# Scores chained in PSUM by key differences, in a differential-attention and ternary feed-forward block

## The chip, the cores and the metric

The kernel runs on one core of a Trainium2 chip. The metric is device time in microseconds. Five engines matter: PE (TensorE, matrix products), DVE (VectorE), ACT (ScalarE), POOL (GpSimd), and SP (SyncE), which issues the DMAs. PE writes its results into eight PSUM banks of 128 x 512 fp32 values; ACT and DVE read them. Each engine works through its own queue in order and waits on semaphores for the others.

## The reference

The input x has 8 batches of 1024 tokens with 512 features. Two residual blocks follow one another:

```python
qkv = layernorm(x) @ w_qkv                       # 16 heads of 32 features
q1, q2 = split(q); k1, k2 = split(k)             # 16 features each
a1 = softmax(q1 @ k1.T / sqrt(32)); a2 = softmax(q2 @ k2.T / sqrt(32))
out = (a1 - lam * a2) @ v                        # per head
out = out / rms(out) * norm_w * (1 - 0.8)
x = x + reorder(out) @ wo
h = bitlinear(layernorm(x), w_fc) + gate * (low-rank term)
x = x + bitlinear(relu(h) ** 2, w_proj)          # weights rounded to -1, 0, 1 times a scale
```

Everything is fp32. The kernel's products of scores use a pair of rounded numbers for each fp32 number (a high part and the rest), laid along the contracted rows.

## The kernel before

A **unit** is one head of one batch for half of the queries (512): 256 units in all, 32 a batch. A unit has eight **key blocks** of 128 keys, and the main loop runs over them two at a time, so a **step** is two blocks and a unit is four steps (`kc` = 0, 2, 4, 6). Everything is computed transposed: a score bank holds 128 keys by 512 queries of one of the two softmax halves (`sm` 0 and 1).

Two streams run beside each other. `max_scores` (L200) computes, 16 blocks ahead (`AHEAD`, L443), the scores with queries along the partitions, and DVE reduces every bank to its negated row maximum (L223). There are four such products and four reductions in a step. The maxima of a unit are turned by PE (`max_turn`, L241, with a transpose at L243), split into high part and rest on DVE, and sent through DRAM into the tile `nms`. `exp_scores` (L264) then computes the scores of a block: first a product of ones with `nms`, which writes minus the maximum into the bank, and then the product of keys and queries on top of it; ACT takes the exponential out of the bank (L284). Each of these products uses 64 of PE's 128 rows, half 0 the lower and half 1 the upper rows, and neighbours of different halves overlap. `values` (L307) multiplies the exponentials of the step before with V, `add_up` (L290) adds them on POOL, and `sums` (L321) turns the sums into denominators on PE.

PSUM's eight banks are three in a ring for the maxima (`ps_mx`, L60), four in a ring called `one` (L61) for the scores and for every other product, and one accumulator. In a step the four maximum products therefore need the first one's bank again for the fourth. In the first call of a step (`apart=True`) ACT copies the first bank to SBUF (L218), and DVE reduces the copy later, after the others.

The order on PE, ACT, DVE and POOL is the program's order; nothing is reordered. In a step the program emits: the first maximum product, the four products of one block with the second maximum product behind them, the four of the other block, POOL's addition, two more maximum products, the **128-row work** that is due, DVE's last reductions, the values, and then the `post` functions (the ACT and DVE work on the results of the 128-row work), in the order in which they were collected.

The 128-row work is: the preparation of the next batch (`prepare`, L410: normalized tiles turned by `advance`, V by `value_tile`, queries and keys by `project`, L152), `max_turn`, the unit's result turned back and normalized (`heads_out`, L329), `sums`, and once in four units the RMS norm (L367 to L384) and the product with `wo` (`output_rows`, L386). One preparation step is taken at `kc` = 0 of each unit, and an extra one at `kc` = 4 of every fourth unit in a batch's second half; a turned tile and a V tile alternate in the first half, and projections follow. A projection is eight matmuls and has a post: ACT writes the high part (L165), DVE the rest (L166), SP stores both into `qk` in DRAM. `load_keys` (L178) and `load_queries` (L187) bring a head's rows back, each doubled. In the last batch there is no next one to prepare; every second unit there (`light`) leaves its last addition to PE. After the attention loop the feed-forward part runs over 16 groups of 512 tokens.

Of the kernel before, what the change touches and what calls it, by code (L numbers as in the profile page):

```python
# [24 lines left out]
def block_phases(  # L25
# [30 lines left out]
    p_mc = ctx.enter_context(tc.tile_pool(name="a_mc", bufs=2))  # L56
    p_tk = ctx.enter_context(tc.tile_pool(name="a_tk", bufs=3))
# [45 lines left out]
    hT_of, v_of, qk_of, og_of = {}, {}, {}, {}  # L103
# [7 lines left out]
    def begin_batch(b):  # L111
        hT_of[b] = big.tile([P, KC, S], F32, tag="hT", name="hT")
        v_of[b] = big.tile([P, NS, E], F32, tag="v", name="v", bufs=2)
        qk_of[b] = dpool.tile([2, E, 2, S], F32, tag="qk", name="qk", bufs=2)

# [36 lines left out]
    def project(b, which, blk, half):  # L152
# [9 lines left out]
        def post():  # L162
# [6 lines left out]
            nc.sync.dma_start(qk_of[b][which, blk * P : (blk + 1) * P, :, tok], pc.bitcast(F32))  # L169
# [4 lines left out]
    tk_of, tq_of = {}, {}  # L174

    def load_keys(g):  # L178
        b, h = divmod(g, H)
        tk_of[g] = p_tk.tile([P, S], F32R, tag="tk", name="tk")  # L180
        src = qk_of[b][1, h * HD : (h + 1) * HD]
        for i in range(2):
            nc.sync.dma_start(
                tk_of[g][i::2].bitcast(F32), src[:, i : i + 1, :].to_broadcast([HD, 2, S])
            )
# [11 lines left out]

    copy_of = {}

    def max_scores(u, i, apart=False):  # L200
# [15 lines left out]
        if apart:  # L216
            copy_of[0] = p_mc.tile([P, 512], F32, tag="mc", name="mc")
            nc.scalar.copy(copy_of[0], mx[0])  # L218
        else:
            product(1)  # L220

        def reduce(kh, sm, src):
            nc.vector.tensor_reduce(  # L223
                nm_of[u][:, kh, sm, c : c + 1], src, AX.X, ALU.max, negate=True
            )

        def post():
            for sm in range(1 if apart else 0, 2):
                reduce(kh, sm, mx[sm])
            if not apart and copy_of:  # L230
                reduce(0, 0, copy_of.pop(0))
# [32 lines left out]
    def exp_scores(u, kc, between=None):  # L264


        if kc % 2 == 0:
            e_of[u, kc // 2] = p_e.tile([P, 2, 2, HS], F32, tag="e", name="e")
        e = e_of[u, kc // 2]
        halves = (1, 0) if between else (0, 1)  # L270
        st = {sm: one_bank() for sm in halves}
        for w, m, cols in (
            (one2, nms[u % 3], slice(0, P)),
            (tk_of[u // 2], tq_of[u], slice(kc * P, (kc + 1) * P)),
        ):
            for sm in halves:
                rows = slice(64 * sm, 64 * sm + 64)
                nc.tensor.matmul(  # L278
                    st[sm], w[rows, cols], m[rows, :], start=(w is one2), stop=(w is not one2)
                )  # L280
        if between:
            between()
        for sm in halves:
            nc.scalar.activation(e[:, kc % 2, sm, :], st[sm], AF.Exp)  # L284
# [22 lines left out]
    def values(u, kc):  # L307
        b, h = divmod(u // 2, H)
        if kc == 0:
            acc_of[u] = ps_acc.tile([P, 512], F32, tag="acc", name="acc")[:, 0 : HS // 2]  # L310
        quarters(
            acc_of[u], v_of[b][:, kc, h * HD : (h + 1) * HD], e_of[u, kc // 2][:, kc % 2],
# [8 lines left out]
    def sums(u):  # L321
        ps = one_bank()
# [87 lines left out]
    def prepare(b):  # L410
# [15 lines left out]
        steps = [(start, False), (lambda: advance(-2), False), (lambda: advance(-1), False)]  # L426
        for t in range(NS):
            steps += [(lambda t=t: advance(t), False), (lambda t=t: value_tile(b, t), True)]
        return steps + [
            (lambda w=which, k=blk, f=half: project(b, w, k, f), True)  # L430
# [12 lines left out]
    AHEAD = 16  # L443
# [7 lines left out]
    with tc.tile_pool(name="a_stage", bufs=1) as stage, tc.manual_schedule(engines=engines):  # L451
# [55 lines left out]
        for i, step in enumerate(steps):  # L507
# [4 lines left out]
            now = [others.pop(0) for _ in range(2 if i < heads + 2 else 1) if others]  # L512
# [8 lines left out]
            if i == heads - 3:  # L521
                load_keys(0)
                load_queries(0)
            if i >= heads:
                um, im = divmod(i - heads, NS)
                if im == 0:
                    if um > 0:
                        load_keys(um // 2 + 1)
# [40 lines left out]
    def prepare_tokens():  # L569
# [24 lines left out]
        return [(lambda i=i: step(i), False) for i in range(-2, 4)]  # L594
# [4 lines left out]
    for v in range(NU):  # L599
        adds.setdefault((v + 1, 2) if light(v) else (v + 2, 0), []).append(v)  # L600
# [524 lines left out]
```

## Time and profile before

| | us |
|---|---|
| median of 3 runs | 5311.46 (5309.91 to 5316.05) |
| the profiled execution's own time | 5314.59 |
| its span | 5312.1 |
| PE busy | 5212.4 |
| POOL busy | 4125.0 |
| DVE busy | 3818.4 |
| ACT busy | 3311.5 |

The span runs from the first to the last instruction; the time around it is the launch. Busy time is the union of an engine's rows: overlapping matmuls count once. The attention loop runs from about 140 to 4236 us, the feed-forward part from there to the end. The profiled core had its full clock for 0.998 of the time. Of one batch (the transposes of the maxima, L243, mark the units) the length is 518.5 to 518.8 us; units of the second half last 15.5, 15.9, 15.6 and 22.6 us in turn, the last with output rows and an extra projection. A row of a group gives busy time, mean length of one in ns, and the engine's idle time just before them with what ended it. A row of the timeline gives start, length, engine, line, operation, and how many were merged.

### The profile page before, as it was taken

The numbers are of one execution on the slowest core, as the hardware profiler recorded it, in microseconds if no ns is written. First come the engines' busy times: TensorE is split into PE (matmuls) and PEld (weight loads), VectorE is DVE, ScalarE is ACT, GpSimd is POOL, SyncE is SP. The second block draws the span as 40 slices with busy tenths as digits, with TensorE's granted clock in tenths as the row PEclk, the third lists the DMA queues.
The fourth block names the chain that finished last, engine by engine and source line by source line (L and its number), as shares of the span: only waits on it lengthen the run. The fifth ranks groups of instructions, "written<-read, shape, count | busy, mean of one in ns | idle before, by whom it ended". The sixth has DMA issues, their size and how long they took to land.

```text
span 5312.1 us, 106552 instructions
## 1 busy us (share of the span) xinstructions
PE 5212.4 (98%) x41522; PEld 3200.8 (60%) x41522; DVE 3818.4 (72%) x7599; ACT 3311.5 (62%) x6518; POOL 4125.0 (78%) x1495
## 2 busy tenths in 40 slices
PE   8999999999999999999999999999999999999999
PEld 4555555555555555555555555555555588888887
DVE  6877787777778777877787778777888645555554
ACT  4776777677767776777677767776777622222221
POOL 0898899889989998999899989998888733333333
PEclk9999999999999999999999999999999999999999
DMA  8112211221121112111211121112211101111111
GB/s 275 48 55 76 71 50 56 75 70 52 56 79 64 52 56 77 64 56 60 77 60 53 65 73 62 52 66 77 97 50 46 60 19 32 32 32 32 32 32 32
DMA packets 185252, 328.54 MB, mean 62 GB/s; under 512 B 33312, under 2 KB 55840, under 8 KB 184112
## 3 DMA queue, kind: packets, MB, share of 16 engines
q1 hardware_dynamic: 183824, 319.12, 18.5%
q8 instruction: 330, 5.41, 0.4%
q0 software_dynamic: 544, 2.10, 0.1%
q14 instruction: 170, 1.39, 0.1%
q10 hardware_dynamic: 384, 0.52, 0.0%
HBM read 209.16 MB, written 112.46 MB: 61 GB/s over the span
## 4 chain that ended last, share of the span: by engine, by line
PE 84%; POOL 8%; ACT 5%; issue 2%; DVE 1%; DMA 0%; SPq 0%; POOLq 0%; DVEq 0%; ACTq 0%
PE acc L301 16%; PE one L278 14%; PE mx L210 12%; PE y L774 8%; PE one L158 8%; PE pf L755 8%; PE one L301 5%; POOL es L296 4%; ACT e L284 4%; PE one L146 4%; PE one L394 4%; PE one L335 2%; POOL es L294 2%; PE pf L759 1%; ACT mc L218 1%
## 5 line engine op out<-in xcount | busy, mean ns | idle before, releaser
L296 POOL TENSOR_TENSOR es<-es,e 128x2048 f32<-128x2048 f32 x495 | 2263.9, 4574 | 51.6 <-ACT e L284 19.7
L223 DVE TENSOR_REDUCE nm<-mx 128x1 f32<-128x512 f32 x3080 | 1990.6, 686 | 319.8 <-PE mx L210 258.4
L284 ACT ACTIVATE e<-one 128x512 f32<-128x512 f32 x4096 | 2132.1, 615 | 24.4 <-PE one L278 15.9
L294 POOL TENSOR_TENSOR es<-e 128x2048 f32<-128x2048 f32 x256 | 1170.9, 4574 | 259.3 <-ACT e L284 259.3
L210 PE MATMUL mx<-tk,tq 64*128 64x512 f32 x4096 | 1362.9, 421 | 1.1 <-DVE nm L223 0.4
L278 PE MATMUL one<-nms,one 64*128 64x512 f32 x4096 | 1177.7, 421 | 31.7 <-ACT e L284 28.5
L301 PE MATMUL acc<-e,v 128*32 128x256 f32 x16384 | 1093.9, 384 | 0.0
L278 PE MATMUL one<-tq,tk 64*128 64x512 f32 x4096 | 1061.5, 392 | 0.0
L210 PEld LDWEIGHTS mx<-tk,tq 64*128 64x128 f32 x4096 | 701.7, 184 | 490.3 <-DVE nm L223 284.9
L218 ACT COPY mc<-mx 128x512 f32<-128x512 f32 x1016 | 598.8, 589 | 311.2 <-PE mx L210 284.4
L764 POOL TENSOR_TENSOR r<-r 128x512 f32<-128x512 f32 x256 | 268.5, 1050 | 640.0 <-ACT r L763 619.8
L301 PEld LDWEIGHTS acc<-e,v 128*32 128x32 f32 x16384 | 451.6, 109 | 443.6 <-issue 166.5
L223 DVE TENSOR_REDUCE nm<-mc 128x1 f32<-128x512 f32 x1016 | 687.2, 676 | 0.0
L763 ACT ACTIVATE r<-pf,s_fc 128x512 f32<-128x512 f32 x256 | 176.4, 689 | 795.4 <-PE pf L759 558.3
L278 PEld LDWEIGHTS one<-tq,tk 64*128 64x128 f32 x4096 | 581.4, 185 | 80.0
L278 PEld LDWEIGHTS one<-nms,one 64*128 64x128 f32 x4096 | 517.3, 184 | 109.5 <-ACT e L284 56.9
L774 PE MATMUL y<-wpr,r 128*128 128x512 f32 x2048 | 524.9, 398 | 3.5 <-DVE r L767 1.5
L767 DVE CAST r<-r 128x512 fp32r<-128x512 f32 x256 | 180.7, 706 | 424.6 <-POOL r L764 422.2
L158 PE MATMUL one<-hT,wqk 128*128 128x512 f32 x1024 | 474.4, 606 | 2.0 <-ACT hT L139 1.5
L774 PEld LDWEIGHTS y<-wpr,r 128*128 128x128 f32 x2048 | 375.8, 188 | 98.7 <-DVE o L784 20.1
L755 PE MATMUL pf<-hTh,wfc 128*128 128x512 f32 x1024 | 398.9, 390 | 0.0
L755 PE MATMUL pf<-hTl,wfc 128*128 128x512 f32 x1024 | 398.7, 389 | 0.0
(139 smaller groups left out, 4562.4 us busy)
## 6 DMA issues: line engine op xcount, KB each, us to landing
qk<-pc SPq DMA_DIRECT2D x128, 512.0 KB
tq<-qk SPq DMA_DIRECT2D x512, 128.0 KB
tk<-qk SPq DMA_DIRECT2D x256, 256.0 KB
xs<-in_L_attn_x SPq DMA_DIRECT2D x64, 256.0 KB
xr<-in_L_attn_x SPq DMA_DIRECT2D x256, 64.0 KB
x_dram<-y SPq DMA_DIRECT2D x64, 256.0 KB
out<-o SPq DMA_DIRECT2D x248, 64.0 KB
nms<-md SPq DMA_DIRECT2D x512, 4.0 KB
```

The source lines that it names most:

```text
L158: nc.tensor.matmul(ps, wqk[:, kc, c0 : c0 + P], hT_of[b][:, kc, tok], start=(kc == 0), stop=(kc == KC - 1),)
L210: nc.tensor.matmul(mx[sm], tq[rows, c * P : (c + 1) * P], tk[rows, kh * 512 : kh * 512 + 512], start=True, stop=True,)
L218: nc.scalar.copy(copy_of[0], mx[0])
L223: nc.vector.tensor_reduce(nm_of[u][:, kh, sm, c : c + 1], src, AX.X, ALU.max, negate=True)
L278: nc.tensor.matmul(st[sm], w[rows, cols], m[rows, :], start=(w is one2), stop=(w is not one2))
L284: nc.scalar.activation(e[:, kc % 2, sm, :], st[sm], AF.Exp)
L294: nc.gpsimd.tensor_add(es_of[u], e_of[u, 0], e)
L296: nc.gpsimd.tensor_add(es_of[u], es_of[u], e)
L301: nc.tensor.matmul(out[32 * g : 32 * g + 32, :], w, e[:, g // 2, (g % 2) * (HS // 2) : (g % 2 + 1) * (HS // 2)], start=start, stop=stop,)
L755: nc.tensor.matmul(pf, w[:, kc, :], hT, start=(kc == 0 and i == 0), stop=False)
L764: nc.gpsimd.tensor_mul(r, r, r)
L774: nc.tensor.matmul(ys[i], r2[:, i * P : (i + 1) * P], prep.wpr[j // (NJ // 2)][:, j % (NJ // 2), :], start=(j == 0 and k == 0), stop=(j == ...
```

## The change

Minus the maxima are multiplied only for a unit's first two blocks. The other six blocks are computed on top of what their bank already holds: the bank of block i holds the scores of block i - 2 minus the maximum, and a product of the queries with the **difference of the keys** of the two blocks turns it into the scores of block i minus the maximum. For that, blocks are taken in the order 0, 4, 1, 5, 2, 6, 3, 7 (`block`), so that both chains go through neighbouring blocks of one half of the keys. A projection of keys now also stores differences: its post copies the product to SBUF, subtracts it shifted by 128 columns, splits the difference into a high part and the rest, and stores these and the first blocks themselves into a second DRAM array, `kd`. `load_steps` brings a head's differences into `td`, once in two units, beside the keys `tk` that the maxima still use.

Since the four banks of `one` now hold scores from a unit's first block to its last, other work can use them only at the unit's end (`kc` = 6): preparation, `max_turn`, `heads_out` and most `sums` go there, and the loads of a next tile (`"pre"`) to `kc` = 2. What must be done elsewhere (output rows, the sums of light units) takes a bank of the maxima's ring. Where more than three posts wait, the first is done ahead of `sums`. The copy of a maximum bank on ACT is gone: DVE reduces all four from PSUM. The maxima run 18 blocks ahead.

```diff
-    p_mc = ctx.enter_context(tc.tile_pool(name="a_mc", bufs=2))
-    p_tk = ctx.enter_context(tc.tile_pool(name="a_tk", bufs=3))
+    p_tk = ctx.enter_context(tc.tile_pool(name="a_tk", bufs=2))
...
-            nc.sync.dma_start(qk_of[b][which, blk * P : (blk + 1) * P, :, tok], pc.bitcast(F32))
+            rows = slice(blk * P, (blk + 1) * P)
+            nc.sync.dma_start(qk_of[b][which, rows, :, tok], pc.bitcast(F32))
+            if which == 0:
+                return
+            kf = p_x.tile([P, E], F32, tag="x", name="kf")
+            nc.scalar.copy(kf, ps)
+            pd = p_pc.tile([P, 2, HS], F32R, tag="pc", name="pd")
+            hi, lo = pd[:, 0, P:], pd[:, 1, P:]
+            nc.vector.tensor_sub(lo.bitcast(F32), ps[:, P:], kf[:, 0 : HS - P])
+            nc.scalar.copy(hi, lo.bitcast(F32))
+            nc.vector.tensor_sub(lo, lo.bitcast(F32), hi.bitcast(F32))
+            k0 = half * HS
+            nc.sync.dma_start(kd_of[b][rows, :, k0 : k0 + P], pc[:, :, 0:P].bitcast(F32))
+            nc.sync.dma_start(kd_of[b][rows, :, k0 + P : k0 + HS], pd[:, :, P:].bitcast(F32))
...
+    def load_steps(g):
+        b, h = divmod(g, H)
+        td_of[g] = p_tk.tile([P, S], F32R, tag="td", name="td")
+        load_doubled(td_of[g], kd_of[b][h * HD : (h + 1) * HD])
...
         product(0)
-        if apart:
-            copy_of[0] = p_mc.tile([P, 512], F32, tag="mc", name="mc")
-            nc.scalar.copy(copy_of[0], mx[0])
-        else:
+        if not apart:
             product(1)
...
         def post():
-            for sm in range(1 if apart else 0, 2):
-                reduce(kh, sm, mx[sm])
-            if not apart and copy_of:
-                reduce(0, 0, copy_of.pop(0))
+            for sm in range(2):
+                nc.vector.tensor_reduce(
+                    nm_of[u][:, kh, sm, c : c + 1], mx[sm], AX.X, ALU.max, negate=True
+                )
...
+    def block(i):
+        return (i % 2) * (NS // 2) + i // 2
...
         halves = (1, 0) if between else (0, 1)
-        st = {sm: one_bank() for sm in halves}
-        for w, m, cols in (
-            (one2, nms[u % 3], slice(0, P)),
-            (tk_of[u // 2], tq_of[u], slice(kc * P, (kc + 1) * P)),
-        ):
+        first = i < 2
+        if first:
+            st_of[i] = {sm: one_bank() for sm in halves}
+        st = st_of[i % 2]
+        cols = slice(block(i) * P, (block(i) + 1) * P)
+        if first:
             for sm in halves:
                 rows = slice(64 * sm, 64 * sm + 64)
                 nc.tensor.matmul(
-                    st[sm], w[rows, cols], m[rows, :], start=(w is one2), stop=(w is not one2)
-                )
+                    st[sm], one2[rows], nms[u % 3][rows, :], start=True, stop=False
+                )
+        for sm in halves:
+            rows = slice(64 * sm, 64 * sm + 64)
+            nc.tensor.matmul(
+                st[sm], td_of[u // 2][rows, cols], tq_of[u][rows, :], start=False, stop=True,
+                skip_group_check=not first,
+            )
...
-    AHEAD = 16
+    AHEAD = 18
...
-        adds.setdefault((v + 1, 2) if light(v) else (v + 2, 0), []).append(v)
-        outs.setdefault((v + 2, 0) if light(v) else (v + 3, 0), []).append(v)
+        adds.setdefault((v + 1, 2) if light(v) else (v + 1, 6), []).append(v)
+        outs.setdefault((v + 1, 6) if light(v) else (v + 2, 6), []).append(v)
...
-            if fill and (kc == 0 or kc == 4 and u % (2 * H) >= H and u % 4 == 0):
-                prepare_step, long = fill.pop(0)
...
-                    later[u, 6] = lambda n=n: rms_squares(n)
-                    later[u + 1, 0] = lambda n=n: rms_sums(n)
-                    later[u + 1, 2] = lambda n=n: rms_apply(n)
-                    later[u + 2, 4] = lambda n=n: output_rows(n)
...
+            if kc == 2 and u < NU:
+                if u % 2 == 0 and u + 2 < NU:
+                    load_steps(u // 2 + 1)
+                if fill and fill[0][1] == "pre":
+                    fill.pop(0)[0]()
+            if kc == 6:
+                if fill and fill[0][1] == "long":
+                    posts.append(fill.pop(0)[0]())
+                if um <= NU:
+                    posts.append(max_turn(um - 1))
+                for v in outs.pop((u, kc), []):
+                    posts.append(heads_out(v))
+                    if v % 4 == 3:
+                        n = v // 4
+                        later[u + 1, 2] = lambda n=n: rms_squares(n)
+                        later[u + 1, 4] = lambda n=n: rms_sums(n)
+                        later[u + 2, 0] = lambda n=n: rms_apply(n)
+                        later[u + 2, 4] = lambda n=n: output_rows(n, mx_bank)
+                if fill and fill[0][1] == "turn":
+                    posts.append(fill.pop(0)[0]())
...
             if reduce:
                 reduce()
+            if len(posts) > 3:
+                posts.pop(0)()
+            for v in adds.pop((u, kc), []):
+                posts.append(sums(v, one_bank if kc == 6 else mx_bank))
```

In the feed-forward part the tile `r2` alternates between the tags `tk` and `td`, four buffers instead of three.

## The prediction

> **What bounds the kernel now.** I read the page's busy line first, then the groups by shape for the two things the change touches, then the busy time of two stretches, then the timeline.
>
> ```profile
> PE 5212.4 (98%) x41522; PEld 3200.8 (60%) x41522; DVE 3818.4 (72%) x7599; ACT 3311.5 (62%) x6518; POOL 4125.0 (78%) x1495
> L223 DVE TENSOR_REDUCE nm<-mx 128x1 f32<-128x512 f32 x3080 | 1990.6, 686 | 319.8 <-PE mx L210 258.4
> L278 PE MATMUL one<-nms,one 64*128 64x512 f32 x4096 | 1177.7, 421 | 31.7 <-ACT e L284 28.5
> ```
>
> PE looks like the only bound, and the products with the maxima (L278, `nms`) cost it 1177.7 us of overlapped rows. That is the tempting reading. The stretches below are the two halves of one batch of the attention loop (16 units each); columns are length, then PE, PEld, DVE, ACT and POOL busy.
>
> ```profile
> 3226.00:3470.00 244.00, 237.34 (x2226) 134.51 (x2227) 197.40 (x406) 189.54 (x374) 238.73 (x84) 1.00 0.17 51
> 3470.00:3742.00 272.00, 271.60 (x2304) 152.22 (x2304) 202.51 (x407) 188.19 (x375) 237.78 (x61) 1.00 0.24 81
> ```
>
> In the first half POOL is busy 238.7 of 244 us: its three 4.6 us additions a unit are the bound. In the second PE is (271.6 of 272), because every unit carries a projection. Only there can PE time be won.
>
> The inside of one step (two key blocks; four steps make a unit):
>
> ```profile
> 2029.10 0.50 PE L210 MATMUL mx<-tk,tq 64*128 64x512 f32 x1
> 2029.10 0.74 PE L278 MATMUL one<-nms,one 64*128 64x512 f32 x2
> 2029.64 0.59 ACT L218 COPY mc<-mx 128x512 f32<-128x512 f32 x1
> 2030.15 1.95 DVE L223 TENSOR_REDUCE nm<-mx 128x1 f32<-128x512 f32 x3
> 2030.39 0.39 PE L210 MATMUL mx<-tk,tq 64*128 64x512 f32 x2
> 2030.71 1.07 PE L301 MATMUL acc<-e,v 128*32 128x256 f32 x16
> 2031.71 0.50 PE L210 MATMUL mx<-tk,tq 64*128 64x512 f32 x1
> ```
>
> A step lasts 2031.71 - 2029.10 = 2.61 us (2.59 to 2.61 elsewhere). Its twelve 64-row products run as six overlapping pairs: the first takes 0.34, the next 0.23 each, so the last two maximum products start at 1.29 (1.26 in other steps); the values start 0.32 later and take 1.0. DVE is nearly as full: four reductions spaced 0.60 to 0.66 give 2.4 to 2.6. What a maximum bank costs when a reduction frees it is seen once, at the loop's start:
>
> ```profile
> 138.71 0.72 PE L210 MATMUL mx<-tk,tq 64*128 64x512 f32 x2
> 139.24 1.29 DVE L223 TENSOR_REDUCE nm<-mx 128x1 f32<-128x512 f32 x2 [1.88 <-PE mx L210]
> 139.98 0.18 PEld L210 LDWEIGHTS mx<-tk,tq 64*128 64x128 f32 x1 [0.52 <-DVE nm L223]
> ```
>
> Product at 138.71, reduction at 139.24 (0.53 later), its first 0.686 done at 139.93, next product into that bank at 139.98 (0.05 later): 1.27 us from a product to the next in the same bank. Last, a unit's end with a projection:
>
> ```profile
> 2036.92 0.27 PE L243 MATMUL one<-ident,nm 128*8 128x128 f32 x1
> 2037.12 0.60 ACT L165 ACTIVATE pc<-one 128x512 fp32r<-128x512 f32 x1 [2.32 <-PE one L158]
> 2037.76 0.69 DVE L166 SCALAR_TENSOR_TENSOR pc<-one,pc 128x512 fp32r<-128x512 f32 x1 [2.48 <-ACT pc L165]
> 2038.36 0.27 DVE L247 CAST mt<-one 8x128 fp32r<-8x128 f32 x1
> 2039.43 0.49 PE L210 MATMUL mx<-tk,tq 64*128 64x512 f32 x1
> 2039.80 0.29 DVE L358 TENSOR_TENSOR og<-one,o 128x128 f32<-128x128 f32 x1
> ```
>
> The next unit starts 2.51 us after the projection's last issue (2036.92), and DVE is free of the posts only 0.66 us after that start.
>
> **The change part by part.**
>
> *Products with the maxima.* 3072 of 4096 go, six pairs a unit, in three of its four steps. Taken from PE's rows alone: 2 x 0.23 = 0.46 us a step, 768 steps, 353 us.
>
> *The ACT copy of one maximum bank (L218) goes, the ring stays at three banks.* A step uses four: the fourth product goes into the first one's bank. Before, that bank was free at 0.53 + 0.59 = 1.12 (ACT), and PE came at 1.26: no wait. Now PE comes at 0.34 + 2 x 0.23 = 0.80, but the bank is free only after the reduction: 0.53 + 0.69 + 0.05 = 1.27. So PE waits 0.47 there, and with it the values queued behind: 1.27 + 0.32 + 1.0 = 2.59 us a step. The saving of 0.46 becomes this wait. DVE keeps up (four reductions at 0.605 = 2.42, plus 0.17 for L235 in one step). I take 0 for the mid-steps; the ends are 0 and -0.46. ACT's 0.59 a step is off the path: four exponentials at 0.52 are 2.07.
>
> *Key differences, in the eight projections of keys per batch.* The post becomes on DVE and ACT: L166, a subtraction from PSUM, a rounding copy on ACT, a second subtraction, and only then the posts of the maxima and of the heads, queued on DVE behind them. Not in the trace at 384 columns; between 256 and 512 columns the rows are 0.42 and 0.69 (DVE), 0.38 and 0.59 (ACT). Middle values: 0.56 + 0.05 + 0.48 + 0.05 + 0.48 (the second at DVE's spacing) = 1.62 later, ends 1.3 and 2.1. DVE is then free 0.66 + 1.62 = 2.28 after the next unit's start, and the fourth product comes at 2.26 + 0.69 + 0.05 = 3.0 instead of 1.27: 1.74 us. (The heads' bank, needed by the next unit's fourth score bank, comes free at 2.3, inside this wait.) Before, the first reduction of a step was of a late copy and nothing waited for it. 8 x 1.74 = 13.9 a batch. For queries' projections DVE is free at 0.66, product at 1.40: 8 x 0.13 = 1.0.
>
> *Moved work.* L373 (0.68) now sits between a mid-step's reductions: the next first reduction is 0.57 late, six times in a batch's heavy units: 3.4. The output rows' bank comes from the three-bank ring, 0.2 x 6 = 1.2. `rms_apply` moves on POOL ahead of another unit's additions, its 4.2 us unchanged; sums come one step earlier, so POOL may lag 2.6 us less.
>
> *Distribution.* All long work is now at unit ends, one a unit: 24 units in a row with it, 8 without. Heavy: 3 x 2.59 + 1.67 to the projection + 3.54 + 2.5 = 15.48; 24 x 15.48 + 8 x 0.5 (four L138 transposes) + 6 x 3.7 (eight L394 matmuls at 0.43 and the switch) = 397.7. The same count for the old second half (16 x 15.48 + 3 x 3.54 + 4 x 3.7 = 273) meets its 272 to 273.5. Light: a unit without a projection is 3 x 2.59 + 1.67 + 2.5 = 11.94 on PE, so 8 x 12.0 + 2 x 3.7 = 103; POOL needs 8 x (3 x 4.6 + 4.2/4) = 119 (L379, L380 and L382 together 4.2, once in four units) plus 3 of statistics, less what it may lag behind; I take 115, nearer POOL's end because the first half above runs at POOL's pace. Sum 512.7, against 518.6 measured between batch starts: -5.9.
>
> *Queues.* SP gets 256 more loads (`td`, 256 KB like `tk`) and 128 more stores of some 0.55 us of issue; the last store of a key projection holds SP 1.6 us longer, with the maxima's store and the queries' load behind it, both due a unit later. The engines' DMA share of 0.17 to 0.24 has room for 96 MB more: 0. If that cover went, each late load would cost a unit its wait of a microsecond or two.
>
> *Sum.* A batch: -5.9 + 13.9 + 1.0 + 3.4 + 1.2 = +13.6. Seven batches prepare another: +95. The last one has no projections but eight of each moved wait: 8 x 0.57 + 8 x 0.2 = +6. The feed-forward part is untouched. The profiled run's own 5314.6 (span 5312.1 and 2.5 around it) + 101 = 5415.6; it lies 3.1 above the median, so **5412 us**.
>
> [...] With the copy kept the fourth product would come at 1.17 by the rows, 0.10 a step better: some 50 us over 24 x 3 x 7 steps.
>
> **The rivals.**
>
> *The key posts don't show* (chance 0.17). DVE idles about 5 us of each projection, which speaks for it; against it, that idle time lies before the projection ends, and the posts need its result. Without 7 x 13.9: 5314, from 5285 to 5345 with the light stretch at 103 to 119.
>
> That the products would not really go is no rival: their loop runs only for a unit's first two blocks.
>
> *The fourth product does not wait* (0.13, the faster side). If its bank were free at 0.80, 0.46 goes from three steps in 24 units: 33 a batch, 7 x (13.6 - 33) = -136, and 32 x 1.38 = -44 plus 6 in the last: 5311 - 174 = 5137. It decides from 0.2 us a step: the product would have to come by about 1.07. DVE's own 2.42 a step leaves only 0.17 of it. Against it stands the one direct reading of 1.27.
>
> *More waits at unit ends* (0.12). If POOL's shorter slack or late maxima cost each unit of a batch 0.4 us more: 5412 + 7 x 32 x 0.4 = 5502. For it: POOL already has 98% in half the units.
>
> **How the numbers follow.** The forecast has 0.58; alone it reaches from 5350 (light stretch 107, key posts 1.3) to 5465 (light 119, posts 2.1). The range takes in the first rival: 5285 to 5490, leaving out the faster case and most of the slowest, 0.2. About 0.2% (5301 to 5322) is what can be told from no change. Faster: 0.13 + 0.05 of the first rival = 0.18; same 0.07; slower 0.75.
>
> **What would show it.** Right: the fourth L210 product of a step 1.27 after the first, waiting for DVE's reduction; steps still 2.6; units after a key projection some 1.7 longer; PE busy falling while its waits for the reductions grow. Wrong: steps near 2.15 to 2.45, or key units no longer than query units. The light stretch (the POOL floor) is the weakest term.

## The result, and the profile after

The changed kernel takes 5845.87 us (median of four runs, 5838.94 to 5848.15) against 5313.2 us for the kernel before (four runs): a ratio of 1.1001, 95% interval 1.0982 to 1.1020. It is slower, as forecast, but by 533 us where 101 were forecast, and far above the range. Its profiled execution took 5846.1 us (span 5844.3), at a mean granted clock of 0.958 instead of 0.998.

From the page of the kernel after: the busy line, and the groups of the reductions, of the products with the maxima and of the output rows; the last line is the output rows of the kernel before. A group row gives busy time, mean ns of one, and the idle time before them with what ended most of it.

```profile
PE 5425.4 (93%) x38450; PEld 3049.7 (52%) x38450; DVE 3980.1 (68%) x7727; ACT 2890.2 (49%) x5630; POOL 4119.7 (70%) x1495
...
L242 DVE TENSOR_REDUCE nm<-mx 128x1 f32<-128x512 f32 x4096 | 2557.5, 683 | 390.7 <-PE one L305 218.1
...
L300 PE MATMUL one<-nms,one 64*128 64x512 f32 x1024 | 370.0, 464 | 209.2 <-DVE mt L261 125.4
...
L425 PE MATMUL mb<-wo_sb,og 128*128 128x512 f32 x504 | 270.6, 687 | 95.6 <-POOL og L413 88.8
```

```profile
L394 PE MATMUL one<-wo_sb,og 128*128 128x512 f32 x504 | 229.8, 598 | 4.1 <-ACT e L284 0.3
```

The products with the maxima did fall from 4096 to 1024 and from 1177.7 to 370.0 us, and yet PE is busy 213 us longer than before, with fewer matmuls. The last two rows say why that can be: the 128x512 matmul of the output rows has a mean of 687 ns here, of 598 before, and of 607 in an experiment below in which PE does not idle ahead of it. Part of PE's time is the same work at half speed: single matmuls of that line take up to 1222 ns in the kernel after, at a median of 592. And two waits stand in the rows that were not there before: for `mt` (the maxima's post, on DVE) and for `og` (`rms_apply`, on POOL).

The busy time of two stretches, one batch (length, PE, PEld, DVE, ACT, POOL, granted clock, DMA share):

```profile
1300.50:1605.00 304.50, 278.55 (x2170) 141.76 (x2169) 213.16 (x432) 170.81 (x334) 258.89 (x90) 0.94 0.20 65
1605.00:1893.30 288.30, 264.42 (x1992) 129.87 (x1991) 211.69 (x402) 156.53 (x308) 219.53 (x55) 0.95 0.26 88
```

A batch is 592.8 us (518.6 before), and now nothing is full in either half: PE 91% and 92%, POOL 85% and 76%. Before, POOL was full in one and PE in the other. Time without a full engine is time spent waiting in turns. Seven batches cost 74 more each; of the last, which prepares nothing, 31 units take 471 against 457.

One step in the middle of a unit, from the timeline:

```profile
1048.34 0.49 PE L231 MATMUL mx<-tk,tq 64*128 64x512 f32 x1
...
1048.68 0.39 PE L231 MATMUL mx<-tk,tq 64*128 64x512 f32 x1
...
1048.87 2.48 DVE L242 TENSOR_REDUCE nm<-mx 128x1 f32<-128x512 f32 x4 [0.23 <-PE one L305]
...
1049.13 0.98 PE L231 MATMUL mx<-tk,tq 64*128 64x512 f32 x2
1049.61 0.18 PEld L231 LDWEIGHTS mx<-tk,tq 64*128 64x128 f32 x1 [0.52 <-DVE nm L242]
...
1050.04 1.07 PE L329 MATMUL acc<-e,v 128*32 128x256 f32 x16
...
1051.04 0.50 PE L231 MATMUL mx<-tk,tq 64*128 64x512 f32 x1
```

The third product starts at 0.79; the fourth has its weights loaded at 1.27, when DVE's first reduction is done, as forecast. But the step is 1051.04 - 1048.34 = 2.70 us, not 2.59. The median over the 430 steps like this one, without products with the maxima and without 128-row work, is 2.71 (before: 2.60 over the 684 steps without 128-row work), with the products at 0.34, 0.80 and 1.28 and the values at 1.71. So the values start 0.43 behind the fourth product, not 0.32: the fourth product now runs alone, with no partner in the other half of PE's rows to overlap with.

A unit's end after a projection of keys, from the timeline:

```profile
1053.04 9.14 POOL L324 TENSOR_TENSOR es<-es,e 128x2048 f32<-128x2048 f32 x2
...
1057.12 0.69 DVE L166 SCALAR_TENSOR_TENSOR pc<-one,pc 128x512 fp32r<-128x512 f32 x1 [3.05 <-ACT pc L165]
...
1057.84 0.59 ACT L176 COPY kf<-one 128x512 f32<-128x512 f32 x1 [0.76 <-DVE pc L166]
...
1058.46 0.56 DVE L179 TENSOR_TENSOR pd<-one,kf 128x384 f32<-128x384 f32 x1 [0.65 <-ACT kf L176]
1058.79 0.50 PE L231 MATMUL mx<-tk,tq 64*128 64x512 f32 x1
1059.05 0.51 ACT L180 CAST pd<-pd 128x384 fp32r<-128x384 f32 x1 [0.62 <-DVE pd L179]
...
1059.60 3.00 DVE L181 TENSOR_TENSOR pd<-pd 128x384 fp32r<-128x384 f32 x1 [0.58 <-ACT pd L180]
...
1063.15 0.79 PE L300 MATMUL one<-nms,one 64*128 64x512 f32 x1 [2.54 <-DVE mt L261]
...
1065.87 1.93 PE L329 MATMUL acc<-e,v 128*32 128x256 f32 x16
```

Three things are to be seen. The two subtractions, of the same 128x384, take 0.56 and 3.00 us. The second one starts inside POOL's addition, which ends at 1053.04 + 9.14 = 1062.18, and ends 0.42 after that. The copy to SBUF does not run beside L166, which reads the same bank: it waits for L166's semaphore and starts 0.03 after its end. And once PE goes on, after 2.54 us of idling, its matmuls take 0.79 instead of 0.50 and its values 1.93 instead of 1.07. The units behind a key projection take 21.9 to 23.4 us, or 25 to 26 where output rows come on top; the other units of that stretch 15.9.

The chain of waits named the two places, summed over the run (total, times, longest):

```profile
PE one L300 <- DVE mt L261: 125.4, 56, 2.8
PE mb L425 <- POOL og L413: 88.8, 28, 6.8
```

56 is 7 x 8: every key projection in the loop. The second, from the timeline:

```profile
1303.26 9.19 POOL L324 TENSOR_TENSOR es<-es,e 128x2048 f32<-128x2048 f32 x2
...
1315.81 1.05 POOL L413 TENSOR_TENSOR og<-og,ss 128x512 f32<-128x512 f32 x1
1316.91 6.41 PE L425 MATMUL mb<-wo_sb,og 128*128 128x512 f32 x8 [6.73 <-POOL og L413]
```

POOL has two additions to do ahead of `rms_apply`; PE comes to the output rows when the second has begun, waits 6.73 us for it, and then takes 6.41 us for eight matmuls that take 3.70 elsewhere. Two units of a batch, 25.5 and 32.6 us long where their neighbours take 12.8 and 16.3, hold such a wait, of 4.0 to 6.8 us. The same two in the kernel before, at their closest within the loop:

```profile
1231.25 1.05 POOL L382 TENSOR_TENSOR og<-og,ss 128x512 f32<-128x512 f32 x1
...
1233.21 3.67 PE L394 MATMUL one<-wo_sb,og 128*128 128x512 f32 x8
```

There POOL is done 0.91 us ahead of PE. In the program five steps lie between `rms_apply` and the output rows before the change (`u + 1`, `kc` 2, to `u + 2`, `kc` 4), and two after it (`u + 2`, `kc` 0 to 4).

### The profile page after: what moved, and what is told of

Same layout as the page of the kernel before. It is cut to its first block, busy times and chain, and to the rows that moved or that the text cites. A ratio compares the mean times of both kernels' runs of the same rounds, so it can differ in the third digit from the quotient of the medians.

```text
span 5844.3 us, 100396 instructions
## 1 busy us (share of the span) xinstructions
PE 5425.4 (93%) x38450; PEld 3049.7 (52%) x38450; DVE 3980.1 (68%) x7727; ACT 2890.2 (49%) x5630; POOL 4119.7 (70%) x1495
## 4 chain that ended last, share of the span: by engine, by line
PE 63%; DVE 14%; POOL 11%; issue 7%; ACT 3%; DMA 0%; SPq 0%; DVEq 0%; POOLq 0%; ACTq 0%
PE acc L329 13%; PE mx L231 11%; DVE nm L242 9%; PE y L811 8%; PE pf L792 7%; POOL es L324 6%; PE one L158 6%; PE mb L425 5%; PE one L146 3%; PE one L329 2%; PE one L305 2%; POOL es L322 2%; PE one L300 2%; POOL ss L411 1%; ACT e L312 1%
## 5 line engine op out<-in xcount | busy, mean ns | idle before, releaser
L242 DVE TENSOR_REDUCE nm<-mx 128x1 f32<-128x512 f32 x4096 | 2557.5, 683 | 390.7 <-PE one L305 218.1
L231 PE MATMUL mx<-tk,tq 64*128 64x512 f32 x4096 | 1680.4, 463 | 77.9 <-DVE nm L242 18.0
L231 PEld LDWEIGHTS mx<-tk,tq 64*128 64x128 f32 x4096 | 736.6, 193 | 938.7 <-DVE nm L242 698.9
L329 PE MATMUL acc<-e,v 128*32 128x256 f32 x16384 | 1145.1, 399 | 0.0
L305 PE MATMUL one<-tq,td 64*128 64x512 f32 x4096 | 1101.8, 432 | 0.0
L305 PEld LDWEIGHTS one<-tq,td 64*128 64x128 f32 x4096 | 550.2, 194 | 49.4 <-ACT e L312 2.6
L300 PE MATMUL one<-nms,one 64*128 64x512 f32 x1024 | 370.0, 464 | 209.2 <-DVE mt L261 125.4
L425 PE MATMUL mb<-wo_sb,og 128*128 128x512 f32 x504 | 270.6, 687 | 95.6 <-POOL og L413 88.8
L166 DVE SCALAR_TENSOR_TENSOR pc<-one,pc 128x512 fp32r<-128x512 f32 x128 | 88.6, 692 | 362.6 <-ACT pc L165 362.6
L300 PEld LDWEIGHTS one<-nms,one 64*128 64x128 f32 x1024 | 157.8, 192 | 303.9 <-DVE mt L261 149.7
```

Of the source, the lines that this page charges most:

```text
L231: nc.tensor.matmul(mx[sm], tq[rows, c * P : (c + 1) * P], tk[rows, kh * 512 : kh * 512 + 512], start=True, stop=True,)
L242: nc.vector.tensor_reduce(nm_of[u][:, kh, sm, c : c + 1], mx[sm], AX.X, ALU.max, negate=True)
L300: nc.tensor.matmul(st[sm], one2[rows], nms[u % 3][rows, :], start=True, stop=False)
L305: nc.tensor.matmul(st[sm], td_of[u // 2][rows, cols], tq_of[u][rows, :], start=False, stop=True, skip_group_check=not first,)
L329: nc.tensor.matmul(out[32 * g : 32 * g + 32, :], w, e[:, g // 2, (g % 2) * (HS // 2) : (g % 2 + 1) * (HS // 2)], start=start, stop=stop,)
L425: nc.tensor.matmul(py, og_of[n][:, c, :], wo_sb[:, c, :], start=(c == 0), stop=(c == KC - 1),)
```

## The experiments

Each was timed against the kernel before, whose median was 5312 to 5315 us each time.

**The second subtraction reads a bank instead of SBUF.** Edit of the kernel after:

```diff
-            nc.vector.tensor_sub(lo.bitcast(F32), ps[:, P:], kf[:, 0 : HS - P])
-            nc.scalar.copy(hi, lo.bitcast(F32))
-            nc.vector.tensor_sub(lo, lo.bitcast(F32), hi.bitcast(F32))
+            nc.vector.tensor_sub(ps[:, P:], ps[:, P:], kf[:, 0 : HS - P])
+            nc.scalar.copy(hi, ps[:, P:])
+            nc.vector.tensor_sub(lo, ps[:, P:], hi.bitcast(F32))
```

> The changed kernel, but the difference of keys is written back into the projection's own PSUM bank, so that the second subtraction (L181, which took 2.0 to 3.3 us in the attention loop and 0.56 us ahead of it) reads one operand from PSUM and one from SBUF. Theory 'blocked operand': L181 stretches because it reads two SBUF operands while POOL adds (each stretched one ends right after a POOL addition). Then it falls to about 0.6 us, units after a key projection (22.9 and 25 to 26 us) lose 2 to 2.5 us directly, and some of PE's half-clock stretches there go too: 8 x 2.2 to 8 x 4.5 us a batch, so 5590 to 5720 us. Rival 'the chain alone': L181's length is only time spent waiting in DVE's queue for something else, and it stays above 2 us wherever its operands are: 5830 to 5850 us.

5672.23 us, ratio 1.0678 (1.0662 to 1.0694): 174 us less than the change. The groups by shape, first of the kernel after, then of this one:

```profile
L181 DVE TENSOR_TENSOR pd<-pd 128x384 fp32r<-128x384 f32 x64 | 155.7, 2433 | 37.0 <-ACT pd L180 37.0
```

```profile
L181 DVE TENSOR_TENSOR pd<-one,pd 128x384 fp32r<-128x384 f32 x64 | 35.7, 558 | 34.8 <-ACT pd L180 34.8
```

The same subtraction falls from a mean of 2433 to 558 ns by taking one operand from PSUM. The waits of L300 for `mt` are no longer among PE's largest, and the units behind key projections come down from about 23 to between 18.7 and 20.2, those with output rows from 25 to 26 to about 23.5. Of the 174 us some 120 are the subtraction's own time (56 in the loop, 2.70 to 0.56 each); the half clock that is told of below falls with it, from 489 to 285 us. With two SBUF operands all 56 in the loop begin during one of POOL's additions, take 1.96 to 3.26 us (2.70 on average) and end 0.41 to 0.42 after it; the eight before the loop, where POOL adds nothing, took 0.56 as well. The rows show when the subtraction stretches; by what mechanism, no run shows.

**The output rows one unit later.** Edit of the kernel after:

```diff
-                        later[u + 2, 4] = lambda n=n: output_rows(n, mx_bank)
+                        later[u + 3, 4] = lambda n=n: output_rows(n, mx_bank)
```

> The changed kernel, but the product with wo is taken one unit later (u + 3 instead of u + 2), so that the RMS factor that POOL works out behind its additions is due a unit earlier than it is needed. Theory 'moved wait': PE's waits for POOL's result ahead of the output rows (88.8 us in PE's rows, 28 of them) and the half-clock stretches that follow (output rows of 6.4 us instead of 3.7) vanish; units of 25.5 and 32 us fall to about 17 and 24: 5700 to 5780 us. Rival 'POOL floor': in that stretch POOL's additions are the bound anyway, and the waits go to the sums or the exponentials: over 5820 us.

5765.29 us, ratio 1.0855 (1.0839 to 1.0871): 81 us less. The six steps that now lie between are enough: the waits for `og` are gone from the list, the eight matmuls take 3.7 us in all 64 places (in the kernel after, 5.2 to 6.7 in 16 of them), and the two long units become 12.3 and 24.4. The group of the output rows:

```profile
L425 PE MATMUL mb<-wo_sb,og 128*128 128x512 f32 x504 | 231.4, 602 | 11.8 <-DVE nm L242 11.6
```

**Both together.**

> The first two experiments together: the difference of keys in PSUM and the output rows one unit later. If the two waits are separate, their gains add up: 5846 - 174 - 81 = 5591, 5570 to 5610 us. If PE, freed of one, waits for the same engine at another place, less than half of the smaller gain is left: over 5630 us.

5576.04 us, ratio 1.0497 (1.0482 to 1.0513). 5845.9 - 174 - 81 would be 5591: the two causes add, with 15 us more than the sum.

**The fourth product behind the values**, in the steps that carry no 128-row work:

```diff
-            reduce = max_scores(um, im + 1) if um < NU else None
+            fourth = None
+            reduce = max_scores(um, im + 1, late=kc != 6) if um < NU else None
+            if reduce and kc != 6:
+                fourth, reduce_late = reduce
+                reduce = None
...
+            if fourth:
+                fourth()
+                reduce_late()
```

> The changed kernel, but in the three mid-steps of a unit the fourth maximum product is issued after the values instead of before them, so that PE has the values to work on while DVE frees the bank. Theory 'ring wait': the mid-step falls from 2.71 us to between 2.42 (DVE's four reductions) and 2.5: 0.2 to 0.3 us in three steps of 32 units, 19 to 28 us a batch where POOL does not bind, so 5640 to 5740 us. Rival 'the wait moves on': the next step's first products wait instead, and the time stays within 30 us of 5846.

5970.31 us, ratio 1.1238 (1.1219 to 1.1257): 124 us more than the change. The step stays at 2.71. The fourth product now overlaps with the next step's first, but the next step's third product waits for the reduction of the one that came late: the products start at 0, 0.57 and 1.28, the values at 1.71, the same places. And each unit's last step, whose two products now both wait, is some 0.7 us longer (units of 15.9, 16.3 and 12.3 become 16.6, 17.0 and 13.0). The theory that the order on PE could get around the ring fell: in both orders a product waits in every step for a reduction.

**Only the products removed, in the kernel before.**

```diff
-        for w, m, cols in (
+        both = (
...
-        ):
+        )
+        for w, m, cols in both if kc < 2 else both[1:]:
...
-                    st[sm], w[rows, cols], m[rows, :], start=(w is one2), stop=(w is not one2)
+                    st[sm], w[rows, cols], m[rows, :], start=(w is one2 or kc >= 2),
+                    stop=(w is not one2),
```

> The kernel before, with only the products with the maxima left out in the last six blocks of a unit (the exponentials there are taken without minus the maximum, so the attention part of the result is another); everything else as it was, the copy of a maximum bank on ACT included. Theory 'steps are full on three engines': ACT's copy and four exponentials take 2.63 us, DVE's reductions 2.4 to 2.6, so the step stays at 2.55 to 2.6 us and the time within 60 us of 5313. Rival 'PE's rows': 0.46 us come off three steps of each unit that PE bounds, half the units and the last batch: 5110 to 5200 us.

5302.38 us, ratio 0.9981 (0.9972 to 0.9990). 3072 of PE's products vanish, with nothing added, and the time falls by 10 us of the 353 that their rows take. A step in the timeline:

```profile
1641.96 0.49 PE L210 MATMUL mx<-tk,tq 64*128 64x512 f32 x1
...
1642.76 0.86 PE L210 MATMUL mx<-tk,tq 64*128 64x512 f32 x2
1643.55 1.07 PE L303 MATMUL acc<-e,v 128*32 128x256 f32 x16
1644.55 0.49 PE L210 MATMUL mx<-tk,tq 64*128 64x512 f32 x1
```

The step is 2.59 us as before: here, with ACT's copy kept, the fourth product comes at 1.17 (median) and alone, the values 0.43 later at 1.60; with the products in, it comes at 1.27, paired, the values 0.33 later at 1.60. The removed work held the step by 0.1 us at most: PE's own queue ended at 1.27, the bank was free at 1.17, and the pairing that is lost takes the difference back.

**The copy on ACT taken out of the kernel before**, as the change does:

```diff
-        if apart:
-            copy_of[0] = p_mc.tile([P, 512], F32, tag="mc", name="mc")
-            nc.scalar.copy(copy_of[0], mx[0])
-        else:
+        if not apart:
             product(1)
...
-            for sm in range(1 if apart else 0, 2):
+            for sm in range(2):
```

> The kernel before with one part of the change alone: ACT's copy of a maximum bank is left out and DVE reduces all four banks from PSUM. PE comes to the fourth product at 1.26 us, the bank is free at 1.27. Theory 'ring': the step grows by 0.05 to 0.15 us (the changed kernel's steps are 2.71), felt where PE binds: 5330 to 5400 us. Rival 'the copy was only ACT's load': steps stay at 2.6 and the time within 10 us of 5312, or falls a little.

5341.45 us, ratio 1.0055 (1.0038 to 1.0071): 29 us more. The step becomes 2.71 here too, with the products at the same 1.28 and the values at 1.71, so the 2.71 of the change comes from taking the copy out and not from the chained scores. That 29 us come of it here and not 768 x 0.11 = 84 fits POOL's pace in the first half of a batch: a batch grows by 3.6 us, its second half by 3.9 and its first half not at all. No run tests this further.

**PE kept busy while it waits for POOL**, first with 14 and 8 filling products, then with 7 and 4:

```diff
+        for _ in range(busy):
+            nc.tensor.matmul(py, ident, wo_sb[:, 0, :], start=True, stop=True)
...
+                        busy = {31: 7, 3: 4}.get((u + 2) % (2 * H), 0) if u + 2 > 2 * H - 4 else 0
```

> The changed kernel, but in the two units of each batch whose output rows wait 6.7 and 4.0 us for POOL, PE multiplies constants into the waiting bank meanwhile (14 and 8 products of 0.43 us); nothing else differs and no wait is shortened. Theory 'clock': PE's granted clock is halved after such an idle stretch, and that, not the wait alone, stretches the rows that follow (output rows 6.4 us instead of 3.7). Then these units get 2.5 to 3 us shorter although PE has more to do: 14 x 2.8, so 5795 to 5820 us, and output rows of 3.7 us there. Rival 'the rows are slow for another reason' (POOL or DMA beside them): output rows stay at 6.4, the time at 5840 to 5860 us.

5875.01 us, ratio 1.1058 (1.1042 to 1.1075). Each filling product shows as two matmul rows here (28 for the 14, 12.28 us where 14 x 0.43 = 6.0 were planned), so they ran past POOL's result; the time says nothing. The output rows behind them fell from 6.4 to 3.6 us all the same. So, with half of them:

> After, with the filling products ahead of the waiting output rows cut to 6.0 and 3.4 us (seven and four products of two passes each), so that they end before POOL's result comes and cost nothing themselves. If the half clock is what PE's idle wait brings on, the output rows (8 matmuls) take 3.6 us instead of 6.4 and the two units of a batch that have the wait lose 2.8 us each: 14 x 2.8 = 39, some 5800 to 5825. If the slow matmuls come from something else than the idle wait: output rows still 6.4, 5840 or more.

5812.79 us, ratio 1.0935 (1.0919 to 1.0951): 33 us less than the change, by work whose result is thrown away. The timeline of this kernel, filling products and output rows:

```profile
1309.33 6.28 PE L425 MATMUL mb<-wo_sb,ident 128*128 128x512 f32 x14
1315.98 3.70 PE L427 MATMUL mb<-wo_sb,og 128*128 128x512 f32 x8 [0.38 <-POOL og L413]
```

POOL's result comes as late in the unit as in the kernel after, but PE has not idled, and the eight matmuls take 3.70 instead of 6.41. In the kernel after, the idle wait on PE cost twice: its 6.73 us, and then 2.7 us in the eight matmuls behind it. In the clock records of the kernel after there are 79 stretches of half clock, 489 us in all, each 3.41, 6.83 or 10.24 us long (the last, at the run's end, 4.68) and beginning during an idle time of PE or at most 2.1 us behind its end; their starts lie on one grid of 3.413 us. Here there are 69 stretches, 364 us; before the change 5 stretches, 22 us. The lengths are one, two and three times 3.41. Waits shorter than that are followed by the half clock too: all 56 of the waits in key units, 1.5 to 2.8 us long, such as the 2.54 us of the key unit above (its stretch: 6.83 us from 1063.0 on). Not every wait is: behind five others of 2.8 to 3.2 us in the kernel after, among them three of L300 for `hT` (from 774.8, 2553.2 and 3147.0 us on), the granted clock stayed at 1.00. What decides this, no run shows.

**The difference work taken out**, with the later output rows:

```diff
-            kf = p_x.tile([P, E], F32, tag="x", name="kf")
-            nc.scalar.copy(kf, ps)
-            pd = p_pc.tile([P, 2, HS], F32R, tag="pc", name="pd")
-            hi, lo = pd[:, 0, P:], pd[:, 1, P:]
-            nc.vector.tensor_sub(lo.bitcast(F32), ps[:, P:], kf[:, 0 : HS - P])
-            nc.scalar.copy(hi, lo.bitcast(F32))
-            nc.vector.tensor_sub(lo, lo.bitcast(F32), hi.bitcast(F32))
...
-            nc.sync.dma_start(kd_of[b][rows, :, k0 + P : k0 + HS], pd[:, :, P:].bitcast(F32))
+            nc.sync.dma_start(kd_of[b][rows, :, k0 + P : k0 + HS], pc[:, :, P:].bitcast(F32))
```

> After, with the output rows a unit later and the key projection's post without the differences: the copy, the two subtractions and the rounding copy are gone, and the second DRAM array gets the keys themselves (the same stores and loads; the result is another). If the two causes found (key posts, output rows' wait) are all that the prediction lacked, the rest of it stands: key units of 15.9 us, a batch near 527, 5380 to 5420 us. If the chained score order costs more in itself, 5450 or more. If the mid-steps were the whole of the rest, 5310.

5406.66 us, ratio 1.0169 (1.0154 to 1.0185). Against the kernel with later rows alone (5765.3) the four instructions cost 359 us, 6.4 for each of the 56 projections. The units behind key projections are 16.0 and 16.4 us, and the last one of a batch 12.4. The loads of the differences, the stores and the chained order remain, and with them the steps of 2.71.

**The copy on ACT put back into that kernel.**

```diff
+        if apart:
+            copy_of[0] = p_mc.tile([P, 512], F32, tag="mc", name="mc")
+            nc.scalar.copy(copy_of[0], mx[0])
+        else:
             product(1)
...
+            for sm in range(1 if apart else 0, 2):
+                reduce(kh, sm, mx[sm])
+            if not apart and copy_of:
+                reduce(0, 0, copy_of.pop(0))
```

> The kernel without the difference work and with later output rows, and with the copy of a step's first maximum bank on ACT put back, its reduction on DVE last, as before the change (the matrix wo shrinks to one quarter, read four times, to make room for the copy's buffer; the result is another). If a step's fourth product waits for DVE's reduction of the first bank, it now comes at 1.17 us instead of 1.27 and the step falls from 2.70 to 2.60: 768 steps at 0.10, 77 us, some 5320 to 5345. If DVE's four reductions are what sets the step, it stays at 2.70 and the time at 5400 or more. If the copy frees the bank without any wait, steps near 2.15 and 5000 to 5100.

5365.04 us, ratio 1.0097 (1.0080 to 1.0114): 42 us less, between the two expectations. Of 683 steps without 128-row work 336 take 2.60 (199 of them a unit's first step), as expected, but 185 take 2.80 and 55 take 2.95. One of 2.81:

```profile
1321.80 0.50 PE L225 MATMUL mx<-tk,tq 64*128 64x512 f32 x1
...
1322.13 0.51 ACT L348 ACTIVATE avs<-acc,one_nlam 128x256 f32<-128x256 f32 x1
...
1322.49 0.64 ACT L233 COPY mc<-mx 128x512 f32<-128x512 f32 x1
...
1323.18 0.50 PE L225 MATMUL mx<-tk,tq 64*128 64x512 f32 x1 [0.19 <-ACT mc L233]
...
1324.61 0.49 PE L225 MATMUL mx<-tk,tq 64*128 64x512 f32 x1
```

Here ACT first empties the accumulator of the unit before, and the copy queues behind it, so the bank is free at 1.38 and not at 1.17. All 185 steps of 2.80 are a unit's second step and have this eviction ahead of the copy; those of 2.95 do not have it, and what lengthens them stays open. In the steps of 2.71 and 2.80 the ring sets the length; which engine frees the bank decides when.

**The preparation spread otherwise, in the kernel before**: first projections over all units without output rows, then, gentler (the edit shown), with one short step a unit and the projections also in three units with output rows.

```diff
-            if fill and (kc == 0 or kc == 4 and u % (2 * H) >= H and u % 4 == 0):
+            ub = u % (2 * H)
+            if fill and (
+                fill[0][1] and (ub % 4 or ub in (16, 20, 24)) if kc == 0
+                else kc == 4 and not fill[0][1]
+            ):
```

> The kernel before with one other edit: the 24 long preparation steps of a batch (V tiles and projections) are spread over all four quarters of the batch, one at the start of each unit that has no output rows, and the short ones go to the middle of a unit. Theory 'two bounds': the first half of a batch runs at POOL's pace (245 us) and the second at PE's (273), so evening out costs neither more and gives 3 x 15.48 + 15.6 + 0.5 = 62.6 us for four units, 500 a batch: 7 x 10 to 7 x 18 us less, 5185 to 5245 us. Rival 'no slack': DVE's and ACT's posts in the first half make up for it, within 20 us of 5312.

> Before, with the preparation spread more evenly but POOL's additions and the statistics left in their places: short steps (turned tile, V tile) one a unit at the third key step, projections at the first step of units that have no output rows. If even spreading of projections over units moves PE's full stretch into POOL's full stretch, a batch of about 514 and 5270 to 5300 us. If POOL's result is again late for the normalization as in the wider spread, 5312 or more.

5330.76 us (ratio 1.0033, 1.0020 to 1.0046) and 5315.58 us (1.0001, 0.9991 to 1.0011). Neither gains; batches of 518.1 to 521.4 and 518.4 to 519.8 us. In the first, the normalization on ACT waits up to 4.59 us for POOL's statistics in one unit of a batch. In the second nothing is late, and still nothing is won: PE is busy 511.3 of 518.6 us there and 511.7 of 518.7 in the kernel before: some 7 us a batch were all that an even spread could win, though POOL looked like the only bound of the first half.

No version tried here beats the kernel before by a measurable time with the whole result.

## Why the prediction was wrong

The direction holds, and the reading of the ring; the size does not. The second and third row below are differences of runs, taken one behind the other (5845.87, 5765.29, 5406.66 us). Of the 93 us left over the kernel before, the first row is a count and the last its remainder:

| | forecast | measured |
|---|---|---|
| products with the maxima and ring of three banks, 768 mid-steps | 0 | 768 x 0.11 = 84, by count |
| key differences in the posts | 97 | 359 |
| output rows and POOL | 0 | 81 |
| all else (distribution, L373, query posts) | 4 | 9, the remainder |

**"I take 0 for the mid-steps"**: the saving became a wait, and the fourth product does come at 1.27 (measured 1.28), as the one row at the loop's start had it. That the removal alone is worth next to nothing is shown with the copy kept (-10 us, the step unchanged). Mis-sized was the next term: "with it the values queued behind: 1.27 + 0.32 + 1.0". The 0.32 was read from a step in which the last two products overlap; a product that waits by itself has no partner, and the values start 0.43 later. 0.11 us a step, 84 us by count. The 0.43 shows in four kernels (the one after, without the products, without the copy, without the difference work), but no run turns it into 84 us: with the copy back 42 us of the 93 go, in the kernel before its absence costs 29. The price of the copy, 0.10 a step in the prediction, was met in the steps where ACT was free, and outdone by ACT's queue in the others.

**"0.56 + 0.05 + 0.48 + 0.05 + 0.48 = 1.62 later"** is the step that failed most. From L166's end to the last subtraction's end it was 1062.60 - 1057.81 = 4.79. The last 0.48 was 3.00: the prediction priced a DVE instruction by its shape and did not ask where its operands lie and what POOL does meanwhile, though POOL's full busy time stood in its own windows. That term is worth 174 us by its experiment (189 with the rows later). The copy to SBUF, for which the sum had nothing, ran after L166 and ahead of the subtraction, 0.65. The rest of 359, some 170 us or 3.0 for each projection where 1.74 were forecast, holds this and the half clock behind the waits that are left. No run separates these two. By the clock records PE was busy at half clock for 139 us in the run with both edits and for 61 in the one without the difference work; taking half of the difference, some 40 of the 170 are the clock (an estimate).

**"the fourth product comes at 3.0 instead of 1.27"** named the wrong instruction. PE was held at the second block's product with the maxima (L300), whose bank is the one that `max_turn` used and L261 frees; of PE's idle time before matmuls only 18 us in the whole run are put down to the ring's banks (in the mid-steps that wait stands in the rows of PEld, beside a matmul that is still running). The prediction had looked at the heads' bank and found it free inside the other wait, and did not look at the bank of the maxima.

**"`rms_apply` moves on POOL ahead of another unit's additions, its 4.2 us unchanged"** looked at what it delays and not at what waits for it: the sum has nothing for PE waiting here. The move leaves two steps instead of five between `rms_apply` and the output rows, some 7.8 us less, and in the kernel before POOL was done only 0.9 to 4.8 us ahead of PE in five of the eight places of a batch. Now POOL still has two additions ahead of it at the end of the stretch without projections, and PE waits up to 6.8 us. The rival of more waits at unit ends (5502, 0.12) had the mechanism, POOL's missing slack, but spread as 0.4 us over every unit; it is two long waits a batch.

**The clock** is in no term. 0.998 before gave no reason to price it, but the two kinds of waits found bring it with them: all 56 in key units and all 13 of 4.0 us and more for POOL's result are followed by it, and the eight matmuls at 6.41 instead of 3.70 are 2.7 us on a wait of 6.7. PE was to be busy for less time, and was busy 213 us longer; it worked for some 399 of the 489 us of half clock, so that about 200 us of its busy time are the clock (an estimate: half of 399).

**Distribution** (-5.9) was small and isn't shown. With the difference work and late rows out, a batch is 530.8: its eight light units 110.9 (forecast 115), its heavy ones 420 against 403 with the small terms. 8 of the 17 are the mid-steps by count, and most of the rest is one unit of 25 us, where the normalization on ACT waits for POOL's statistics (up to 7.6 us).

The rivals: that the key posts do not show is refuted by 359 us; that the fourth product does not wait, by 1.28 in the kernel after. The lower ends of two ranges do not follow from their own terms: a light stretch of 107 with key posts of 1.3 gives 5338 and not 5350, and 103 without the key posts 5230 and not 5285. The result lies far above all of them.

## What to carry to other kernels

Before counting removed work as a gain, find in the timeline what its step waits for next; here a ring of banks gave back all of it, since the step was set by the way from a product over the reduction to the next product in its bank. Price an added DVE instruction by where its operands lie and by what POOL does at that time (here 0.56 us or 2.70), and try one operand from PSUM where POOL is busy (here 0.56 again). When a change moves two dependent steps closer, read from the trace how much time the first has to spare. A wait that leaves PE idle can be paid again in the matmuls behind it (here 2.7 us behind one of 6.7): look in the clock records for what such waits bring, add that to them, or fill them with matmuls (here 33 us less).

## What the runs showed of the hardware

- A DVE subtraction of 128x384 with both operands in SBUF took 0.56 us in all eight places where POOL was quiet and 2.70 us on average (up to 3.26) in all 56 during POOL's additions of SBUF tiles, ending 0.41 to 0.42 us behind each; with one operand in PSUM (the first experiment) it took 0.56 in all 64. POOL's additions kept their 4.55 us.
- After idle stretches PE ran at half clock, for one, two or three times 3.41 us (the last stretch, at the run's end, 4.68): 79 times, 489 us, in the kernel after. It followed all 56 waits for `mt` (1.5 to 2.8 us) and all 13 of 4.0 us and more for `og`, and none of five others of 2.8 to 3.2 us. Filling the idle time with products whose result was not used made the kernel 33 us faster.
- The values start 0.43 us after a 64-row product that runs alone, and 0.33 after one that overlaps with a product in the other half of the rows. It is small, and by count 84 us here.
